# Accumulator banks and a split second layer for the last MLPs, a head set up in timed steps, and a new order of the last slots

## The chip, the cores and the metric

The kernel runs on one core of a Trainium2 chip. The metric is the device time in microseconds (us) of that core. TensorE is called PE here, VectorE DVE, ScalarE ACT, GpSimd POOL and SyncE SP.

## The reference, cut to what matters

The input x has the shape (4, 64, 64, 256), all in float32. Two layers follow one another.

```python
# layer 0: attention over the 4096 pixels of each image
q, k, v = x @ wq + bq, x @ wk + bk, x @ wv + bv          # 32, 32 and 256 columns
x = gamma * softmax(q @ k.T) @ v + x
# layer 1: a deformable 3x3 convolution (DCNv3, 16 groups) and an MLP, both with residuals
h  = ln(x)
xp = h @ inproj_w + inproj_b                              # what is sampled
d  = gelu(ln(depthwise_conv3x3(h)))
offset, mask = d @ off_w + off_b, softmax(d @ mask_w + mask_b)
s  = sum over 9 taps of mask * bilinear(xp, position + offset)
x  = x + s @ outproj_w + outproj_b
h  = ln(x)
x  = x + gelu(h @ fc1_w + fc1_b) @ fc2_w + fc2_b          # 256 -> 1024 -> 256
```

## The kernel before, in words

**Units and slots.** Each image is cut into 16 units of 256 pixels, 64 units in all. The work is cut into small steps, each a closure that issues a few instructions, and every step has a due time. A slot is 60 units of that time. Unit s has its attention in slot s and its `front` (residual, layer norm, input projection) in slot s+1. Convolution and sampling work on blocks v = 0 to 64, which are shifted by half a unit, so that the first and the last have one tile of 128 pixels and the others have two. Block v has its `plan` (convolution, offsets, masks, weights) in slot v+1, and its `sample` (weighted sums over a 5x5 window on DVE) and `back` (output projection, layer norm and MLP) in slot v+2. The last three blocks, 62 to 64, use `summing` in place of `sample`: part of the adding is then done on PE (`sum`, line 1093). A `far` step at the end repairs, through gathers, up to one sample in each of 128 rows that fell outside the window.

**The order.** `whole` (line 1372) collects all steps with their due times, from the table `WHEN` and, for the last slots, from the table `LATE` (from line 399), sorts them and calls them. Four engines (PE, DVE, ACT and POOL) execute their instructions strictly in that order. SP is not among them: it issues nearly all DMAs, in an order that the scheduler of the framework finds. The due times set an order only; nothing waits for a clock.

**The head.** Before the first step the kernel loads `raw_qk`, then, three times, the weights of offsets and masks into a buffer `raw` of one slot (lines 164 to 170, on SP), which `ordered` (lines 153 to 161) copies on DVE into `om_w` and `om_b` with another order of columns. The next load of `raw` has to wait for the copy before. POOL writes zero borders to the padded image `xp` in DRAM (lines 179 to 187, 16 DMAs) and zero halves (lines 201 to 203, 4 DMAs), and POOL and DVE together fill small tables (`numbers`, lines 212 to 241). Then the projections of the 16 units of the first image run one after another: load `xs` (line 617), transpose on PE (line 316), copy on ACT (line 624), keys on PE (line 630), key bias on ACT with a store `qd` from the two-slot buffer `qT` (lines 638 to 645), values on PE (line 651), value bias on DVE (line 659). `xs` has 8 slots then. Weights of the later stages are loaded on ACT's queue, one step each.

**The tail.** `finish` (line 1126) is the shared end of a block: transpose, output projection, layer norm, then eight `hidden` steps (line 1167; each fills one 128-row piece of the hidden layer in PSUM), eight `gelu` steps (line 1175, ACT reads that bank), and `narrowed` (line 1182), which multiplies all eight pieces with fc2 in one go. `back` (line 1211) and `far_round` (line 1249) use it. The PSUM pool `ps` has two banks with the tag `m`, shared by transposes, projections, `hidden` and `narrowed`. Four banks `e0` to `e3` belong to the attention energies, and two, `acc0` and `acc1` (pool `ps_a`), to the attention output; once the last attention is over, nothing uses these two.

Of the kernel before, what the change touches and what calls it, by code (L numbers as in the profile page):

```python
# [16 lines left out]
def tile_attention_dcnv3_block(  # L17
# [76 lines left out]

    def loaded(t, src, now=False):
        if now:
            nc.scalar.dma_start(t, src)
        else:
            loads.append(lambda: nc.scalar.dma_start(t, src))
# [62 lines left out]

    for k in range(C // P):
        raw = p1.tile([P, 2, NOM], F32, tag="om", name=f"raw_{k}")[:, 0, :]
        nc.sync.dma_start(raw[:, : 2 * S], off_w[k * P : (k + 1) * P, :])
        nc.sync.dma_start(raw[:, 2 * S :], mask_w[k * P : (k + 1) * P, :])
        ordered(om_w[:, k, :], raw[:, : 2 * S], raw[:, 2 * S :])
    raw = p1.tile([P, 2, NOM], F32, tag="om", name="raw_b")[:, 0, :]
    nc.sync.dma_start(raw[:, : 2 * S], off_b.partition_broadcast(P))
    nc.sync.dma_start(raw[:, 2 * S :], mask_b.partition_broadcast(P))  # L170
    ordered(om_b, raw[:, : 2 * S], raw[:, 2 * S :])
# [6 lines left out]
    for b in range(B):  # L178
        for y in (0, H + 2):
            nc.gpsimd.dma_start(  # L180
                xp[b, y : y + 2].rearrange("y w c -> (y w c)").rearrange("(p f) -> p f", p=P),
                zeros[:, : 2 * WP * C // P],
            )
        for w in (0, W + 2):
            nc.gpsimd.dma_start(
                xp[b, 2 : 2 + H, w : w + 2, :].rearrange("y w c -> y (w c)"), zeros[:H, : 2 * C]
            )

# [12 lines left out]
    for v in (0, UN):  # L201
        nc.gpsimd.dma_start(amd_[v, :, 1], zeros[:, :S])
        nc.gpsimd.dma_start(omd_[v, :, 1], zeros[:, :NOM])
# [14 lines left out]
    tab = p1.tile([P, WIN * C], F32, tag="acc", name="tab")  # L218
    byp = tab[0:1, : 6 * S].rearrange("p (s f) -> p s f", f=3)
    numbers(byp[:, :, 0], [[0, 2 * KP], [1, G]], 0)  # L220
    numbers(byp[:, :, 1], [[0, 2], [1, 3], [0, 3 * G]], -1)
    numbers(byp[:, :, 2], [[0, 6], [1, 3], [0, G]], -1)
    nc.gpsimd.dma_start(tab_s.rearrange("(o s) f -> o (s f)", o=1), tab[0:1, : 6 * S])
    tab = p1.tile([P, 2 * S], F32, tag="mk", name="tab_b")
    byt = tab[0:1, : 4 * UN].rearrange("p (s f) -> p s f", f=2)
    numbers(byt[:, :, 0], [[H + 4, B], [0, NT]], 0)
    numbers(byt[:, :, 1], [[0, B], [2, NT]], 0)
    nc.gpsimd.dma_start(tab_t.rearrange("(o s) f -> o (s f)", o=1), tab[0:1, : 4 * UN])
    tab = p1.tile([P, 2 * S], F32, tag="mk", name="tab_c")
    numbers(tab[0:1, :], [[1, 2 * S]], 1)  # L230
    nc.gpsimd.dma_start(tab_n.rearrange("(o s) -> o s", o=1), tab[0:1, :])

    where = gp.tile([P, 3], F32, name="where")
    numbers(where[:, 0:1], [[0, 1]], 0, 1)
    for r in range(2):
        numbers(where[r * W : (r + 1) * W, 1:2], [[0, 1]], 0, 1)
        nc.vector.memset(where[r * W : (r + 1) * W, 2:3], float(r))
    rev = gp.tile([P, PN], F32, name="rev")
    numbers(rev, [[-1, PN]], PN)
    g16 = gp.tile([P, G], F32, name="g16")  # L240
    numbers(g16, [[1, G]], 0)
# [69 lines left out]
    def transposed(src, name, n=2, pool=None, tag="m"):  # L311

        pt = (pool or ps).tile([P, C // P, 256], F32, tag=tag, name=f"pt_{name}")
        for k in range(C // P):
            for i in range(n):
# [57 lines left out]
            "narrowed0": 102.2, "narrowed1": 106.29, "end": 106.65,  # L373
# [7 lines left out]
            "hidden6": 52.93, "gelu6": 53.21, "hidden7": 53.49, "gelu7": 53.77, "narrowed0": 54.05,  # L381
            "end": 54.33,
# [17 lines left out]
        "attention": {  # L400
            60: {"e2": 41.63, "w7": 60.7, "x2": 61.55, "e3": 66.3, "w11": 68.16, "w10": 72.05, "x3": 77.04,
                "w4": 92.63, "w12": 96.73, "w14": 126.44, "w13": 147.54, "w6": 149.16, "w9": 151.58,
                "w8": 162.58, "w15": 163.18},
            61: {"load": 73.15, "e0": 77.73, "x0": 99.75, "e1": 104.68, "w0": 119.31, "x1": 120.96,
                "w4": 128.82, "w7": 135.45, "e2": 139.75, "w5": 140.73, "x2": 142.59, "w6": 144.13,
                "w9": 144.35, "e3": 145.78, "w11": 147.04, "w10": 148.04, "x3": 148.67, "w3": 150.79,
                "w13": 152.23, "w14": 153.3, "w2": 155.04, "w1": 159.09, "w12": 159.2, "w8": 161.6,
                "w15": 162.84},
            62: {"load": 99.58, "e0": 109.75, "x0": 110.1, "e1": 115.56, "w0": 118.27, "w2": 120.32,
                "x1": 120.74, "w6": 125.15, "e2": 126.82, "w5": 128.98, "x2": 130.87, "w7": 131.07,  # L410
                "e3": 132.81, "w11": 137.28, "w10": 140.15, "w1": 141.18, "x3": 141.21, "w3": 142.52,
                "w14": 145.25, "w4": 147.03, "w13": 147.58, "w12": 147.88, "w8": 148.09, "w9": 149.05,
                "w15": 151.71},
            63: {"load": 96.28, "e0": 109.66, "x0": 111.02, "w0": 116.5, "w1": 120.49, "e1": 121.69,
                "x1": 130.68, "w4": 132.65, "w5": 134.09, "e2": 139.76, "w2": 143.15, "w3": 145.56,
                "w6": 148.75, "x2": 149.1, "w10": 151.15, "e3": 151.17, "w7": 152.54, "w8": 159.2,
                "x3": 160.16, "w14": 161.32, "w12": 166.1, "w9": 172.0, "w13": 173.2, "w11": 173.78,
                "w15": 178.59},
        },
        "plan": {  # L420
            60: {"tap3": 42.14, "tap4": 45.5, "tap5": 45.93, "tap6": 48.85, "tap7": 56.79, "tap8": 69.29,
                "turn": 71.67, "stats": 84.78, "shift": 119.53, "norm": 125.14, "turn2": 134.12,
                "gelu": 136.3, "heads0": 139.79, "heads1": 139.85, "bias0": 140.11, "bias1": 141.55,
                "hat0": 143.63, "hat2": 145.22, "mask_exp": 149.39, "hat1": 152.25, "sums": 155.5,
                "nearer": 155.85, "invert": 159.93, "weigh": 161.42, "near": 162.49, "mask0": 163.69,
                "bounds": 164.12, "product0": 169.57, "y_copies0": 169.58, "mask1": 170.65, "y0": 170.84,
                "product1": 173.04, "carry": 176.72, "y_copies1": 176.81, "y1": 177.14, "x_copies": 177.7,
                "x": 179.94, "count": 186.05},
            61: {"tap0": 134.62, "tap1": 137.24, "tap2": 142.14, "tap3": 143.54, "tap4": 145.54,
                "tap5": 147.02, "tap6": 147.16, "tap7": 151.6, "tap8": 153.16, "turn": 155.38,  # L430
                "stats": 159.07, "shift": 163.55, "norm": 165.46, "turn2": 169.08, "gelu": 169.8,
                "heads0": 171.11, "bias0": 173.2, "heads1": 173.5, "bias1": 174.96, "mask_exp": 175.54,
                "sums": 176.03, "hat0": 176.77, "hat2": 179.12, "invert": 179.39, "hat1": 181.33,
                "weigh": 182.69, "nearer": 182.7, "carry": 184.49, "near": 184.56, "mask0": 186.43,
                "product0": 189.28, "mask1": 189.69, "y_copies0": 189.79, "y0": 189.8, "product1": 191.98,
                "y_copies1": 192.03, "y1": 193.12, "bounds": 193.14, "x_copies": 195.14, "x": 197.47,
                "count": 222.68},
            62: {"tap0": 130.69, "tap1": 130.86, "tap2": 132.89, "tap3": 137.61, "tap4": 138.36,
                "tap5": 140.21, "tap6": 143.86, "tap7": 145.27, "tap8": 146.85, "turn": 149.25,
                "stats": 154.57, "shift": 157.76, "norm": 160.13, "turn2": 162.96, "gelu": 163.59,  # L440
                "heads0": 170.06, "bias0": 170.97, "heads1": 171.09, "bias1": 171.17, "mask_exp": 171.28,
                "hat0": 174.71, "hat2": 175.31, "sums": 176.21, "carry": 179.99, "hat1": 180.81,
                "invert": 182.18, "nearer": 182.58, "weigh": 183.33, "near": 185.92, "mask0": 190.13,
                "mask1": 193.9, "product0": 196.16, "y_copies0": 201.23, "y0": 201.65, "product1": 204.17,
                "y_copies1": 207.73, "y1": 208.43, "x_copies": 210.39, "x": 210.97, "count": 221.66,
                "bounds": 346.38},
            63: {"tap0": 141.15, "tap1": 142.22, "tap2": 142.73, "tap3": 143.79, "tap4": 145.1,
# [147 lines left out]
                "summed0": 541.21},  # L595
        },
        "checks": {
            66: {"range": 530.02, "left": 563.34, "largest": 1080.93},
        },
    }  # L600

# [449 lines left out]
    def sample(v, wns, sps):  # L1051
# [71 lines left out]
        return d  # L1123


    def finish(x1, sp, name, n=2, after=None):
        m = n * P
        st = {}

# [366 lines left out]
```

## Time and profile before

| | |
|---|---|
| median of 3 runs | 3838.01 us (3837.57 to 3839.95) |
| the profiled execution | 3837.92 us |
| its span | 3835.8 us |
| PE busy | 3789.8 us, 99% of the span |
| DVE busy | 3401.7 us, 89% |
| ACT busy | 2199.0 us, 57% |
| POOL busy | 312.9 us, 8% |
| last attention matmul ends | about 3663 us |

The profiled execution lies 0.09 us under the median, and 2.1 us of it lie outside the span. A row of a table by stage gives, for a stretch of the span, the busy time of each engine with the number of instructions in brackets, the granted clock of PE as a share of full speed, the share of the 16 DMA engines' time in use, and what they moved. A row of a timeline gives the start, the duration, the engine, the line, the operation with output and input, the number of instructions, and in brackets the idle time before it with what ended that.

### The profile page before, as it was taken

How to read it: one execution, taken by the hardware profiler on the slowest of the kernel's cores; microseconds unless marked ns; L12 is line 12 of the kernel's file. 1: busy time of each engine (PE TensorE's matmuls, PEld its weight loads, DVE VectorE, ACT ScalarE, POOL GpSimd, SP SyncE). 2: the span in 40 equal slices, each digit the busy share in tenths (PEclk: the TensorE clock that was granted, in tenths of full speed). 3: DMA queues.
4: the chain of work that ended last, by engine and by line, in shares of the span. 5: the costliest groups of instructions: out<-in, count | busy, mean ns of one | idle time of the engine just before them, and what ended most of it. 6: DMA issues, size and time to landing. Idle time of an engine off the chain costs nothing.

```text
span 3835.8 us, 56185 instructions
## 1 busy us (share of the span) xinstructions
PE 3789.8 (99%) x20466; PEld 3139.2 (82%) x20466; DVE 3401.7 (89%) x6199; ACT 2199.0 (57%) x4261; POOL 312.9 (8%) x444
## 2 busy tenths in 40 slices
PE   8999999999999999999999999999999999999988
PEld 7788888888888888888888888888888888888867
DVE  2599899999998998998998999999999999999995
ACT  4556556565565565565565565655655565555543
POOL 1000000000000000000000000000000000000021
PEclk9999999999999999999999999999999999999999
DMA  5333333334343333333533333333344333333331
GB/s 151 91 102 90 96 96 93 99 90 139 97 112 92 102 92 90 106 92 90 149 99 105 97 92 99 91 95 97 100 127 112 91 86 88 98 84 84 88 93 51
DMA packets 231789, 378.03 MB, mean 99 GB/s; under 512 B 32880, under 2 KB 181936, under 8 KB 231504
## 3 DMA queue, kind: packets, MB, share of 16 engines
q1 hardware_dynamic: 221408, 367.46, 34.5%
q10 hardware_dynamic: 8512, 3.43, 0.4%
q8 instruction: 163, 2.67, 0.3%
q0 software_dynamic: 1584, 3.47, 0.3%
q14 instruction: 122, 1.00, 0.1%
HBM read 251.69 MB, written 122.56 MB: 98 GB/s over the span
## 4 chain that ended last, share of the span: by engine, by line
PE 96%; DVE 3%; DMA 1%; ACT 0%; issue 0%; SPq 0%; ACTq 0%; DVEq 0%
PE acc L744 46%; PE ph L1170 11%; PE pmlp L1187 11%; PE e L719 7%; PE po L885 5%; PE pout L1145 3%; PE pp L801 3%; PE pv L651 3%; PE pkq L630 1%; DVE pw L1064 1%; PE pt_p L316 1%; PE pc L861 1%; PE pt_f L316 1%; PE pt_s L316 1%; PE pt_b L316 1%; PE pt_x L316 1%
## 5 line engine op out<-in xcount | busy, mean ns | idle before, releaser
L744 PE MATMUL acc<-V,ex 128*128 128x257 f32 x8192 | 1900.9, 382 | 0.2
L744 PEld LDWEIGHTS acc<-V,ex 128*128 128x128 f32 x8192 | 1532.0, 190 | 264.5 <-issue 64.8
L1064 DVE TENSOR_TENSOR pw<-win,wn 128x1280 f32<-128x1280 f32 x640 | 933.8, 1486 | 9.5 <-ACT wn L1008 1.9
L1072 DVE TENSOR_TENSOR pw<-pw,pw 128x1280 f32<-128x1280 f32 x492 | 731.9, 1488 | 0.1
L732 ACT ACTIVATE ex<-e 128x512 f32<-128x512 f32 x1024 | 529.3, 602 | 63.0 <-PE e L719 54.2
L1170 PE MATMUL ph<-hT_b,f1w 128*128 128x256 f32 (+1 forms) x2080 | 493.2, 380 | 6.3 <-ACT gT L1178 2.8
L1187 PE MATMUL pmlp<-f2w,gT 128*128 128x256 f32 x2048 | 462.7, 379 | 1.3 <-DVE x1b L1152 1.1
L1170 PEld LDWEIGHTS ph<-hT_b,f1w 128*128 128x128 f32 x2080 | 381.9, 190 | 82.8 <-issue 18.9
L848 DVE SCALAR_TENSOR_TENSOR cv<-hs,dw,cv 128x256 f32<-128x256 f32 (+1 forms) x1076 | 429.9, 467 | 7.9 <-ACT cv L844 1.3
L1187 PEld LDWEIGHTS pmlp<-f2w,gT 128*128 128x128 f32 x2048 | 384.2, 190 | 51.8 <-DVE x1b L1152 1.4
L288 ACT ACTIVATE xn_p<-pc,nm_p,rstd_p 128x256 f32<-128x256 f32 x128 | 65.4, 560 | 554.1 <-DVE nm_p L280 551.2
L1178 ACT ACTIVATE gT<-ph,f1b 128x256 f32<-128x256 f32 (+1 forms) x520 | 236.5, 468 | 254.8 <-PE ph L1170 253.3
L719 PE MATMUL e<-qs,kT 32*128 32x256 f32 x4096 | 296.3, 401 | 0.7 <-ACT ex L732 0.7
L719 PEld LDWEIGHTS e<-qs,kT 32*128 32x128 f32 x4096 | 186.7, 184 | 72.3 <-issue 63.3
L732 ACT ACT_TABLE_LOAD x182 | 233.5, 1283 | 3.0
L274 POOL TENSOR_SCALAR rstd_p<-mv_p 128x2 f32<-128x2 f32 (+1 forms) x65 | 76.1, 1171 | 1703.4 <-DVE mv_p L272 1632.4
L885 PE MATMUL po<-om_w,ge 128*128 128x432 f32 x512 | 196.6, 527 | 0.7 <-ACT ge L878 0.7
L974 DVE TENSOR_TENSOR pr<-hat 128x1296 f32<-128x1296 f32 x128 | 192.7, 1505 | 0.6 <-DVE nm_b L280 0.5
L1178 ACT ACT_TABLE_LOAD x124 | 159.1, 1283 | 2.1
L878 ACT ACTIVATE ge<-pt_p,bd,gd 128x256 f32<-128x256 f32 (+1 forms) x130 | 66.0, 558 | 157.0 <-PE pt_p L316 157.0
L885 PEld LDWEIGHTS po<-om_w,ge 128*128 128x128 f32 x512 | 96.9, 190 | 71.1 <-issue 63.3
L894 DVE TENSOR_TENSOR om<-po,om_b 128x432 f32<-128x432 f32 x128 | 77.3, 605 | 87.3 <-PE po L885 87.3
(219 smaller groups left out, 3883.1 us busy)
## 6 DMA issues: line engine op xcount, KB each, us to landing
win<-xp SPq DMA_DIRECT2D x536, 320.0 KB, 4.1
omd<-om SPq DMA_DIRECT2D x63, 432.0 KB, 2.5
xs<-in_x_dram SPq DMA_DIRECT2D x64, 256.0 KB, 5.4
x<-in_x_dram SPq DMA_DIRECT2D x64, 256.0 KB, 2.7
x1d<-x SPq DMA_DIRECT2D x64, 256.0 KB, 3.2
xp<-xq SPq DMA_DIRECT2D x128, 128.0 KB, 2.4
x1b<-x1d SPq DMA_DIRECT2D x63, 256.0 KB, 2.8
spd<-sp SPq DMA_DIRECT2D x63, 256.0 KB, 2.1
```

The costliest lines, as they stand in the source:

```text
L316: nc.tensor.transpose(pt[:, k, i * P : (i + 1) * P], src[:, i, k * P : (k + 1) * P], ident)
L719: nc.tensor.matmul(es[r][:, jj, :], lhsT=self.kT[2 * g + jj][rows4(r), :], rhs=self.qs[rows4(r), :], start=True, stop=not self.general,)
L732: nc.scalar.activation(ex, self.es[r], AF.Exp)
L744: nc.tensor.matmul(self.acc[i], lhsT=ex[:, jj, i * P : (i + 1) * P], rhs=V[t // 2][:, t % 2, :], start=(g == 0 and r == 0 and jj == 0), st ...
L848: nc.vector.scalar_tensor_tensor(dst, src, dw[:, k, j : j + 1], dst, ALU.mult, ALU.add)
L885: nc.tensor.matmul(st["po", i], lhsT=st["ge"][:, k, i * P : (i + 1) * P], rhs=om_w[:, k, :], start=(k == 0), stop=(k == 1),)
L974: nc.vector.tensor_mul(pr.rearrange("p a b c d g -> p a b (c d g)"), hat[:, :, i, 1, :].unsqueeze(1).to_broadcast([P, 3, 3, S]), hat[:, :, ...
L1064: nc.vector.tensor_mul(st[r].rearrange("p d (g c) -> p (d g) c", c=GC), src.rearrange("p d (g c) -> p (d g) c", c=GC), wns[v][:, i, r] .re ...
L1072: nc.vector.tensor_add(st[0], st[0], st[r])
L1170: nc.tensor.matmul(ph[:, :m], lhsT=f1w[:, k, c * P : (c + 1) * P], rhs=st["hT"][:, k, :m], start=(k == 0), stop=(k == 1),)
L1178: nc.scalar.activation(st["gT"][:, c, :m], st["ph", c][:, :m], AF.Gelu, bias=f1b[:, c : c + 1])
L1187: nc.tensor.matmul(po, lhsT=st["gT"][:, c, i * P : (i + 1) * P], rhs=f2w[:, c, :], start=(c == 0), stop=(c == NH - 1),)
```

## The change

1. **Free banks.** `finish` gets an argument `last`. It is set for blocks 63 and 64 and for `far`. There, `hidden` takes its bank from a list of two, `acc0` and `acc1`, and `gelu` gives it back. The ring still has two banks, but it no longer shares them with transposes and projections.
2. **Split second layer.** Where `last` is set and the block has one tile (block 64 and `far`), the one step `narrowed0` becomes eight steps `part0` to `part7`, one for each piece of the hidden layer, with due times of their own. The matmuls are the same.
3. **Head in steps.** The three loads of `raw` with their copies, the borders, the halves and the tables are no longer issued ahead of the first step but become steps of their own: load and copy at -24 and -10, at -9 and 5, at 6 and 20; borders at -8, 1, 10 and 19; halves at 28; tables at 32. The projection of unit u of the first image has its value bias at about 3.6u - 59.5, so that the first copy stands between the value biases of units 13 and 14 in DVE's order, and the second and third after the last of them. The first energies of the attention are due at -5.06.
4. **New order.** All of `LATE` is replaced: the due times of the steps of slots 59 to 66.

```diff
+    head = []
+    def head_raw(t, offs, masks, dst):
+        st = {}
+        def load():
+            st["raw"] = raw = p1.tile([P, 2, NOM], F32, tag="om", name="raw_om")[:, 0, :]
+            nc.sync.dma_start(raw[:, : 2 * S], offs)
+            nc.sync.dma_start(raw[:, 2 * S :], masks)
+        head.append((t, load))
+        head.append((t + 14.0, lambda: ordered(dst, st["raw"][:, : 2 * S], st["raw"][:, 2 * S :])))
     for k in range(C // P):
-        raw = p1.tile([P, 2, NOM], F32, tag="om", name=f"raw_{k}")[:, 0, :]
-        nc.sync.dma_start(raw[:, : 2 * S], off_w[k * P : (k + 1) * P, :])
-        nc.sync.dma_start(raw[:, 2 * S :], mask_w[k * P : (k + 1) * P, :])
-        ordered(om_w[:, k, :], raw[:, : 2 * S], raw[:, 2 * S :])
+        rows = slice(k * P, (k + 1) * P)
+        head_raw(-24.0 + 15.0 * k, off_w[rows, :], mask_w[rows, :], om_w[:, k, :])
+    head_raw(6.0, off_b.partition_broadcast(P), mask_b.partition_broadcast(P), om_b)
...
+    for b in range(B):
+        head.append((-8.0 + 9.0 * b, lambda b=b: borders(b)))
...
+    head.append((28.0, halves))
...
+    head.append((32.0, tables))
...
+    spare = [0, 1]
-    def finish(x1, sp, name, n=2, after=None):
+    def finish(x1, sp, name, n=2, after=None, last=False):
...
         def hidden(c):
-            st["ph", c] = ph = ps.tile([P, 256], F32, tag="m", name=f"ph_{name}_{c}")
+            if last:
+                st["bank", c] = k = spare.pop(0)
+                ph = ps_a.tile([P, C + 1], F32, tag=f"acc{k}", name=f"ph_{name}_{c}")
+            else:
+                ph = ps.tile([P, 256], F32, tag="m", name=f"ph_{name}_{c}")
+            st["ph", c] = ph
...
+            if last:
+                spare.append(st["bank", c])
...
+        def part(c):
+            if c == 0:
+                st["pm"] = ps.tile([P, 2, C], F32, tag="m", name=f"pmlp_{name}")
+            nc.tensor.matmul(
+                st["pm"][:, 0, :], lhsT=st["gT"][:, c, :P], rhs=f2w[:, c, :],
+                start=(c == 0), stop=(c == NH - 1),
+            )
...
+            steps += [(t, len(steps) + i, fn) for i, (t, fn) in enumerate(head)]
```

In the new order of the last block, PE does hidden 0, 1 and 6, part 0, hidden 7, 3, 4 and 2, part 1, hidden 5, and parts 2 to 7; before, it did eight hidden steps and then `narrowed0`. Parts 6 and 7 of `far` stand between the last transpose of block 64 and its first hidden step.

## The prediction

> **What bounds the kernel.** I read the page's first part, then a table by stage. PE is busy 99% of the span, and from 260 to 3500 us without a gap, so no step there can be made shorter by another order.
>
> ```profile
> PE 3789.8 (99%) x20466; PEld 3139.2 (82%) x20466; DVE 3401.7 (89%) x6199; ACT 2199.0 (57%) x4261; POOL 312.9 (8%) x444
> ```
>
> ```profile
> 0.00:20.00 20.00, 12.15 (x43) 9.64 (x44) 5.07 (x39) 5.65 (x11) 12.36 (x27) 1.00 0.80 254
> 20.00:40.00 20.00, 16.53 (x85) 13.83 (x84) 7.87 (x20) 8.12 (x20) 3.91 (x13) 1.00 0.83 247
> ...
> 80.00:100.00 20.00, 20.00 (x125) 16.10 (x124) 0.00 (x0) 10.70 (x19) 0.00 (x0) 1.00 0.03 9
> ...
> 3600.00:3660.00 60.00, 59.88 (x321) 48.51 (x320) 59.02 (x115) 28.17 (x56) 8.41 (x11) 1.00 0.33 87
> 3660.00:3700.00 40.00, 31.34 (x128) 23.60 (x127) 36.94 (x82) 20.09 (x43) 8.21 (x8) 0.91 0.27 74
> 3700.00:3720.00 20.00, 16.94 (x80) 13.88 (x78) 19.45 (x62) 3.81 (x8) 4.95 (x7) 1.00 0.29 68
> 3720.00:3740.00 20.00, 17.88 (x80) 13.76 (x78) 20.00 (x42) 12.01 (x23) 2.44 (x2) 1.00 0.52 149
> ```
>
> The change adds and removes no PE work: eight parts hold the matmuls of one `narrowed0`. What it can win is PE's idle time, 3835.8 - 3789.8 = 46 us. By stage: 7.85 + 3.47 = 11.3 us up to 40 us; 6.7 us between 60 and 260 us, which the change does not touch; some 17 us between 3663 and 3825 us; and 10.8 us after PE's last matmul, which stay. In 3600 to 3760 us DVE is full, so there PE waits for DVE, not for banks. That last fact limits the new order most.
>
> **The head.** The timeline of PE shows three waits after the start:
>
> ```profile
> 21.86 1.99 PE L651 MATMUL pv<-wv_s,xT 128*128 128x256 f32 x8 [1.42 <-DVE V L659]
> ...
> 28.04 1.13 PE L630 MATMUL pkq<-xT,wkq 128*128 128x256 f32 x4 [0.72 <-ACT xT L624]
> ...
> 32.66 1.13 PE L630 MATMUL pkq<-xT,wkq 128*128 128x256 f32 x4 [1.32 <-ACT xT L624]
> ```
>
> The first has this cause: DVE stands in `ordered` until the bias loads land (20.11 us), with V's add queued behind. The others come from SP. There the reload of `raw` waited for a DVE copy and was issued at 14.43, with two loads of `xs`, further ones and the first store `qd` behind it; `qd` went out at 19.26, though its `qT` was written by 12.4. ACT needed that slot of `qT` and waited for the store:
>
> ```profile
> 26.16 0.73 ACT L638 ACTIVATE kT<-pkq,bkq 32x128 f32<-32x128 f32 x2 [5.91 <-DMA qd<-qT]
> ```
>
> With the three `raw` loads out of the way, both holds go: 1.42 + 0.72 + 1.32 = **-3.46 us**. What is late next is the store `qd` itself: by my reading it is issued near 16.5, behind the `xs` load that waits for the third unit's transpose (15.44 + 0.60), and landing takes 2.4 us in the median and 6.4 in this case (25.7 - 19.3). So it lands at 19 to 23, and ACT needs the slot at 20 to 21; I leave 0.2 us for it. **Head: -3.3 us.**
>
> PE's start hardly moves. The first `xs` load may go out 1.05 us earlier (1.75 for 2.80), but the values of unit 0 wait for `wv_s` (issued on ACT's queue at 4.61, landed at 11.86). More `xs` loads are then in flight beside it. The nearest row is the span of landing times of 256 KB loads in this head, 3.3 to 8.2 us, so `wv_s` could land between 3.9 us earlier and 1.0 later; I take no change, since its own row is 7.2. Bounds of the head: the start -2 (past that, ACT's first copy at 8.46 and `bv_s` bind) to +1, the waits -3.46 to 0.
>
> [...]
>
> **What moves at no cost.** The borders and halves: POOL has nothing ahead of them in its own order (its next work is `rstd_f` at 106.7 us), so their new due times delay them by nothing, and they stay in the way as now. The tables: ten DVE casts (about 2.6 us) and ten iotas now follow DVE's last value bias, in 65 to 100 us, where DVE does nothing (0.00 busy in 80 to 100). Without that cover they cost their ping-pong from 24.6 to 38 us, some 13 us of DVE. The copies into `om_w` and `om_b` take 6 x 0.40 us, two of them between value biases that stand 3.03 us apart and last 0.69. Their reloads on SP wait for DVE; if SP's order puts later `qd` stores behind one, ACT waits as at 39.81 (2.2 us), where PE lost nothing. `om_w` is first read near 130 us.
>
> **The tail, after the last attention (3663 us).** I wrote out both orders and summed rows.
>
> 1. *To the last `front`.* PE's next need from DVE is the transpose of `xn_f`. Between, PE has 13.4 us before (seven hidden of 0.865, one transpose 0.44, two `narrowed` of 3.46) and 12.1 after (six hidden, two `narrowed`). DVE has 18.3 us from L767 to L280 before and 14.3 after (two multiplies or adds and one product of 1.4 each fewer, `stats` 1.0 more, small ones either way). But `end` of block 59, which needs `narrowed1`, and one `across` now stand just ahead of that `shift`, so PE's gap is 0.55 + 0.6 + 0.6 + 0.1 + 1.0 = 2.9 us. The row before:
>
> ```profile
> 3682.70 1.40 PE L316 MATMUL pt_f<-ident,xn_f 128*128 128x128 f32 x4 [3.02 <-ACT xn_f L288]
> ```
>
> DVE must first have done 4 us more by 3663 than now, and it had 6.5 idle us since 3500. If it has, -1.5; if not, +1.1. I take 0.
>
> 2. *3689 to 3711.* Idle before: 0.91 + 1.11 + 0.56 + 0.56 + 1.15 + 1.82 = 6.1. After, by the walk: project-out directly behind its transpose (ACT's copy, 0.9), a bank freed by DVE's store (0.9), hidden directly behind its transpose (1.1), `gelu2` of block 60 queued on ACT behind `x_copies` of plan 62, which wait for DVE's `y1` (3.1), and the transpose of plan 63 for the last tap (1): 7.0, so **+0.9** (-2.2 if `y1` is early).
>
> 3. *3711 to 3745.* Before 1.11 + 0.66 + 0.35 + 1.13 = 3.3. After: `narrowed0` of block 61 waits for a bank that DVE frees late (2.6), and small ones (0.7): 3.3. **0**, between -2 and +1.
>
> 4. *3745 to 3825, the part that the new steps serve.* The wait for `hT_b` ahead of the last MLP (0.55 at 3815.95) is covered by two parts of `far` (2 x 0.43), and a wait of 0.30 for `sT` by hidden steps: -0.85. The last MLP now:
>
> ```profile
> 3815.95 4.79 PE L1170 MATMUL ph<-hT_b,f1w 128*128 128x128 f32 x32 [0.55 <-ACT hT_b L296]
> 3820.75 3.72 PE L1187 MATMUL pmlp<-f2w,gT 128*128 128x256 f32 x16
> ```
>
> At the rate of `ph_f` (0.89 for eight) the 32 would take 3.5 us: 1.3 are lost in the ring of two banks. The new ring also has two, so the waits stay, but part 0 and part 1 fill 2 x 0.43 of them: -0.9 (0 to -1.3). Parts 2 to 7 stand behind the last hidden step, where `narrowed0` stood.
>
> **Tail: 0 + 0.9 + 0 - 0.85 - 0.9 = -0.85 us** by the walk. A walk of this kind adds every new wait singly, and some fall together. Going through to the end in one piece (DVE and PE side by side from the last `front`), I get 141 us against 143.1 measured, so -2.1. I take the mean, **-1.5**, with ends -9 and +6.
>
> One price I can't settle: behind the wait of 3.02 us the granted clock is half, and `pp` takes 3.78 us in place of 1.73.
>
> ```profile
> 3682.70:3689.00 6.30, 5.37 (x13) 3.41 (x13) 4.23 (x10) 4.94 (x13) 0.00 (x0) 0.50 0.12 42
> ```
>
> That costs (1.40 - 0.44) + (3.78 - 1.73) = 3.0 us per such gap; 1.8 us at 3710 cost nothing like it. My gaps of 2.9, 3.1 and 2.6 lie near the edge: -3 to +6 us, inside the ends above.
>
> [...]
>
> **Sum:** 3837.9 (the profiled execution) - 3.3 - 1.5 = 3833.1; it stands 0.1 under the median, so 3833.2, a change of -0.13%.
>
> **Rivals.** Measurement of this kernel tells a change of about 0.2% (7.7 us) from none.
>
> - *As above*, 3833: both parts work but small. Chance 0.50.
> - *More is won*: the start is 1.5 us earlier, the holds go (-3.5), and the new order gets DVE's 4 us done early (-1.5), hides the wait on `x_copies` (-3), keeps the last front's gap short of the half clock (-3): -12.5, so 3825. For it: 14.9 us of PE idle between 3663 and 3745 are there to be had, DVE has 6.5 idle us ahead. Against: DVE at 59.0 of 60. Chance 0.42.
> - *Slower*: DVE comes late to the last `front`. The order asks 4 us more of it there; if it is 8 us late instead, this passes through (DVE is full until 3760), and two gaps beyond 3 us pay the half clock: +8 + 6 - 1.75 - 3.3 = +9, so 3847. It decides from about 7 us late. Against: DVE's remaining work there is 122 us after and 126 before. Chance 0.08.
> - *The change doesn't do what it says*: borders and ring unchanged, SP still holds `qd` behind another wait, tail by the walk: -0.85, so 3837. It is part of the first case's chance.
>
> **Chances.** Faster by over 0.2% (under 3830.3): the second case, and a little of the first, 0.43. Within: 0.49. Slower: 0.08. Range: 3821 (the second case with 4 us more of its bounds) to 3841 (the first with the head lost and the walk's upper bounds).
>
> **What would show it.** Right: no PE wait on V or `xT` in 20 to 33 us, the first energies near 62 us in place of 65.3; PE's last matmul 1 to 3 us earlier relative to the last `front`; hidden and part rows mixed in the last 10 us; DVE full from 3600 to 3760. Wrong: energies still at 65 (SP holds `qd`), or earlier than 60 (the start moved); PE idle of 3663 to 3745 under 9 us or over 20; half clock in more than one stretch there.

## The result, and the profile after

The changed kernel takes 3833.75 us (median of 22 runs, 3831.99 to 3837.05), the kernel before 3838.61 (22 runs, 3837.01 to 3842.84): a ratio of 0.9986, with a 95% interval of 0.9980 to 0.9993, or -4.9 us. The forecast was 3833.2. The profiled execution took 3833.11 us, its span 3831.2.

The page's first part of the changed kernel, and its table by stage:

```profile
PE 3790.6 (99%) x20466; PEld 3141.2 (82%) x20466; DVE 3401.8 (89%) x6199; ACT 2203.0 (58%) x4265; POOL 313.8 (8%) x444
```

```profile
0.00:20.00 20.00, 11.86 (x42) 9.15 (x43) 4.75 (x35) 5.42 (x11) 12.26 (x27) 1.00 0.88 304
20.00:40.00 20.00, 18.90 (x100) 16.46 (x99) 4.25 (x7) 10.54 (x25) 0.00 (x0) 1.00 0.84 211
...
3660.00:3700.00 40.00, 30.98 (x116) 23.82 (x115) 37.90 (x94) 17.34 (x39) 11.80 (x13) 0.83 0.26 78
3700.00:3720.00 20.00, 19.87 (x94) 16.37 (x93) 19.02 (x56) 8.43 (x18) 7.30 (x6) 1.00 0.32 85
```

PE idles less in 20 to 40 us (1.1 us in place of 3.5) and in 3700 to 3720 us (0.1 for 3.1), and the clock is lower around 3680 (0.83 for 0.91). The timeline of PE in the head, and the row of ACT that holds it:

```profile
12.25 3.78 PE L686 MATMUL pv<-wv_s,xT 128*128 128x256 f32 x8 [1.41 <-DMA wv_s<-in_L_conv_wv_dram]
...
26.95 1.13 PE L665 MATMUL pkq<-xT,wkq 128*128 128x256 f32 x4 [1.10 <-ACT xT L659]
...
62.62 1.15 PE L754 MATMUL e<-qs,kT 32*128 32x256 f32 x16
```

```profile
25.83 0.47 ACT L679 ACTIVATE qT<-pkq,bkq 32x256 f32<-32x256 f32 x1 [3.43 <-DMA qd<-qT]
```

The wait on V is gone, one wait on `xT` is left, and the first energies stand at 62.62 for 65.30. In the last slots:

```profile
3678.18 0.33 PE L335 MATMUL pt_f<-ident,xn_f 128*128 128x128 f32 x1 [2.09 <-ACT xn_f L307]
...
3679.95 3.78 PE L836 MATMUL pp<-inw,hT_f 128*128 128x256 f32 x8 [0.66 <-ACT hT_f L315]
...
3696.61 5.13 PE L1213 MATMUL ph<-hT_b,f1w 128*128 128x256 f32 x16 [3.30 <-ACT gT L1221]
...
3739.50 8.86 PE L1232 MATMUL pmlp<-f2w,gT 128*128 128x256 f32 x32 [1.69 <-DVE x1b L1189]
```

```profile
3811.86 1.85 PE L1213 MATMUL ph<-hT_b,f1w 128*128 128x128 f32 x12
3813.55 0.60 PE L1240 MATMUL pmlp<-f2w,gT 128*128 128x256 f32 x2
...
3816.92 2.76 PE L1240 MATMUL pmlp<-f2w,gT 128*128 128x256 f32 x12
```

The gap ahead of the last front is 2.09 us, shorter than forecast, and `pp` still takes 3.78. The last MLP runs without a wait. On this one profile the sum looks right in its parts too: head -2.7 (forecast -3.3), tail -2.1 (forecast -1.5). The experiments show that this agreement is luck.

### The profile page after: what moved, and what is told of

Read it like the earlier page. It is cut to its first block, busy times and chain, and to the rows that moved or that the text cites. A ratio compares the mean times of both kernels' runs of the same rounds, so it can differ in the third digit from the quotient of the medians.

```text
span 3831.2 us, 56200 instructions
## 1 busy us (share of the span) xinstructions
PE 3790.6 (99%) x20466; PEld 3141.2 (82%) x20466; DVE 3401.8 (89%) x6199; ACT 2203.0 (58%) x4265; POOL 313.8 (8%) x444
## 4 chain that ended last, share of the span: by engine, by line
PE 92%; DVE 3%; issue 0%; ACT 0%; POOL 0%; DVEq 0%; ACTq 0%; POOLq 0%
PE acc L779 44%; PE ph L1213 11%; PE pmlp L1232 11%; PE e L754 7%; PE po L920 5%; PE pout L1182 3%; PE pp L836 3%; PE pv L686 2%; PE pkq L665 1%; DVE pw L1099 1%; DVE cv L883 1%; PE pt_p L335 1%; PE pt_s L335 1%; PE pt_b L335 1%; PE pc L896 1%; PE pt_f L335 1%
## 5 line engine op out<-in xcount | busy, mean ns | idle before, releaser
L754 PEld LDWEIGHTS e<-qs,kT 32*128 32x128 f32 x4096 | 186.2, 184 | 72.8 <-issue 64.9
```

What stands on the lines that cost most here:

```text
L754: nc.tensor.matmul(es[r][:, jj, :], lhsT=self.kT[2 * g + jj][rows4(r), :], rhs=self.qs[rows4(r), :], start=True, stop=not self.general,)
```

## The experiments

Medians are of 8 or 11 runs, beside 12 to 33 of the kernel before in the same series (3838.55 to 3838.76). The table cuts each profile in two: from the first energies to the last front's transpose (`pt_f`), and from there to `pt_any`, PE's last matmuls; "half spans" are explained below the third experiment.

| kernel | first energies | to `pt_f` | to the end | half spans (60 to 80 us / tail) | median |
|---|---|---|---|---|---|
| before | 65.30 | 3617.40 | 141.70 | 0 / 2 | 3838.61 |
| changed | 62.62 | 3615.56 | 141.43 | 0 / 5 | 3833.75 |
| head_only | 63.60 | 3619.16 | 141.68 | 1 / 2 | 3838.36 |
| raw_only | 64.36 | 3621.27 | 142.18 | 2 / 3 | 3841.21 |
| tail_only | 64.13 | 3617.79 | 138.36 | 1 / 1 | 3833.73 |
| old_order | 65.48 | 3619.44 | 141.16 | 1 / 3 | 3838.88 |
| banks_no_split | 65.29 | 3617.83 | 140.85 | 1 / 2 | 3836.91 |
| gelu_early | 66.71 | 3617.88 | 139.58 | 1 / 2 | 3834.21 |
| fill | 65.51 | 3618.86 | 138.23 | 1 / 2 | 3835.59 |
| qT4 | 62.64 | 3617.85 | 138.87 | 1 / 2 | 3834.19 |
| qd_on_act | 64.45 | 3620.58 | 140.04 | 2 / 2 | 3836.28 |
| start | 62.92 | 3616.41 | 140.04 | 0 / 2 | 3832.60 |
| best3 | 61.37 | 3618.30 | 138.86 | 1 / 2 | 3833.62 |
| borders_late | 57.59 | 3615.54 | 141.46 | 0 / 5 | 3828.67 |

**1. The halves apart: head_only, tail_only, raw_only.** `head_only` is the kernel before with the head in steps; `tail_only` the changed kernel with the head issued first, as before; `raw_only` is `head_only` with only the `raw` loads in steps.

```diff
 head_only:  old LATE, and no last=...
 tail_only:  -        head.append((t, load))
             +        load()
             (and the same for the other four head.append)
 raw_only:   head_only, with borders(b), halves() and tables() called in place
```

> The head in timed steps alone; banks, parts and the order of the last slots as before. My theory: the head is worth 2.7 us by itself (first energies 65.30 to 62.62 us in the two profiles), because the reloads of the raw weights no longer stand in SP's order ahead of the qT stores nor in DVE's ahead of the V adds; the last slots then take what they took before, so the time is 3838.6 - 2.7 = 3835.9 us, first energies at 62.6, and from there to PE's last matmul 3759.7 us as before. Rival: the head gains nothing of its own at the end because a later wait (the transposes between 60 and 260 us, or the last slots) takes it back: 3838 us with energies at 62.6. Second rival: the order of the last slots is worth all of it and the head shifts with the run: energies at 65.

> Banks, parts and the new order of the last slots alone; the head issued ahead of the first step as before. My theory: -2.1 us (from the first energies to PE's last matmul 3757.6 us after for 3759.7 before): 3836.5 us, first energies at 65.3. The sum with the other half then adds up to the whole change, -4.9. Rival: the two halves help one another (the DMA rows or DVE's state at 3600 us differ), so that this half alone gives under 1 us or over 4.

> Only the three loads of the raw weights with their copies become timed steps; borders, halves and tables stand ahead of the first step, and the last slots are as before. My theory: all of the head's gain comes from these three, so the first energies are at 62.6 within 0.5 and the time is 3835.9 us. Rival: the casts of the tables on DVE (ten, with ten iotas on POOL, from 24.6 to 38 us before) held V adds too, or the small writes of the borders held loads; then the energies come at 63.5 to 65 and half of the gain or more is missing.

Measured against the kernel before: `head_only` 1.0000 (0.9991 to 1.0009), `tail_only` 0.9989 (0.9980 to 0.9998), `raw_only` 1.0005 (0.9996 to 1.0014). So the last slots bring all of the 4.9 us that can be seen. The head brings none that can be told: 0.4 us without the new order and 0.0 beside it. Taken run by run, the mean differences are -0.3 us (95% interval -1.6 to 1.2) and -0.4 (-1.9 to 0.9). My theory of -2.7 for the head lies outside both and fell, and that of -2.1 for the tail with it. The first energies tell why one profile misled: with the same new head they came at 62.62, 63.60, 65.48, 65.51, 66.71 and 65.29 (mean 64.9), with the old head at 65.30 and 64.13 (64.7). The profiled execution of the changed kernel was the earliest of six. Its wait on `xT` was also the shortest of the six; in the four with waits of 2.5 us or more the granted clock then fell to half between 26 and 34 us. The theory on `raw_only` fell too (energies at 64.36, no gain). Its median is 2.8 us over `head_only`; the two intervals above overlap, but run by run the mean difference is 2.2 us (0.6 to 3.8), so something seems lost where borders, halves and tables stay ahead. What it is stays open.

**2. The order and the split apart: old_order, banks_no_split.**

```diff
 old_order: changed kernel, old LATE, with
 66: "part0": 756.0, "part1": 863.2, "part2": 884.1, "part3": 942.92 ... "part7": 943.32   (block 64)
 66: "part0": 631.85 ... "part7": 632.55                                                   (far)
 banks_no_split: "part7": 1123.25 -> "narrowed0": 1123.25, "part7": 781.47 -> "narrowed0": 781.47
```

> The head in timed steps, the free banks and the parts, but with the old order of the last slots; part 0, 1 and 2 of the last block stand behind gelu 6, 2 and one more in the old order, parts 3 to 7 where the one step stood. My theory: the new order of 3663 to 3745 us was worth nothing (its losses and gains cancel), and the banks and parts alone give 0.9 of the last slots' 2.1 us (the last MLP 9.45 to 8.6 us), the rest being the wait on hT_b and the ring that the order hides: 3838.6 - 2.7 - 0.9 = 3835.0 us. Rival: the order is what gains, and banks and parts give nothing without it: 3835.9 us and a last MLP of 9.4 us. Second rival: the new order loses, and this kernel is faster than the changed one: under 3833.

> The changed kernel without the split: the second layer of block 64 and of far is one step again, where part 7 stands. All else is the changed kernel's. My theory: the split is worth the waits that the parts fill (hT_b 0.55, sT 0.30, two parts of the ring's waits 0.9): 1.0 to 1.8 us, so 3834.8 to 3835.5 us, and from the last gelu to the end of the second layer 3.5 us in place of 2.8. Rival: ACT's gelus bind that stretch whatever PE does; then only the parts behind the last gelu count, and the loss is under 0.5 us.

`old_order` has the ratio 0.9997 (0.9988 to 1.0006): without the new order, banks and parts show nothing in the median, though its last MLP (first `ph` to `pt_any`) took 7.91 us for 8.45 before. My theory of 3835.0 fell; the first rival was right on the time, not on the last MLP. `banks_no_split` lost 3.2 us against the changed kernel, for the 1.0 to 1.8 of my theory. By the table 1.35 of them stand behind `pt_f`, against the mean of the five profiles with equally many half spans and the parts (gelu_early, qT4, qd_on_act, start, best3: 139.5); where the rest is, the profiles don't show. Its timeline shows what the parts had covered:

```profile
3812.29 0.44 PE L335 MATMUL pt_b<-ident,xn_b 128*128 128x128 f32 x2 [1.01 <-ACT xn_b L307]
...
3816.02 4.56 PE L1213 MATMUL ph<-hT_b,f1w 128*128 128x128 f32 x32
3820.42 3.62 PE L1232 MATMUL pmlp<-f2w,gT 128*128 128x256 f32 x16
```

`pt_b` waits 1.01 us for `xn_b`, where otherwise parts of `far` stand. The MLP itself takes 7.95 us, nearly what it takes with parts (7.75), for 8.45 before: in these profiles most of its gain comes with the free banks, little with parts inside it. The new order without the free banks wasn't tried: there, as I read the order, hidden steps of one block stand among transposes and hidden steps of others, and with two shared banks a step would wait for a bank that only a later step frees.

**3. The half clock: fill.** Behind the same wait of 1.69 us `pmlp` took 8.86 us in the changed kernel's profile and 7.17 in that of `tail_only`. A table in steps of 0.05 us shows why: in each profile the clock changes only on a grid of 3.41 us of its own. In the changed kernel it turns to half at 166.69, 3679.01, 3696.08 and 3740.45 us, which lie 1029, 5 and 13 whole steps of 3.413 us apart; the half stretches that its trace records up to PE's last matmul last 3.413, 10.240, 3.413 and 3.413 us, those of the kernel before 6.827 and 6.827. Cut on that grid:

```profile
3675.61:3679.02 3.41, 1.15 (x7) 0.52 (x5) 2.85 (x7) 1.10 (x2) 0.00 (x0) 1.00 0.23 78
3679.02:3682.43 3.41, 2.75 (x8) 2.04 (x7) 3.00 (x19) 3.06 (x7) 1.26 (x2) 0.50 0.24 77
...
3692.67:3696.09 3.42, 0.64 (x3) 0.21 (x2) 3.42 (x12) 0.46 (x3) 0.92 (x2) 1.00 0.00 0
3696.09:3699.50 3.41, 2.89 (x7) 2.36 (x8) 3.41 (x9) 1.30 (x4) 0.00 (x0) 0.50 0.23 77
...
3737.05:3740.46 3.41, 1.52 (x7) 1.14 (x7) 3.41 (x9) 0.58 (x3) 0.00 (x0) 1.00 0.00 0
3740.46:3743.87 3.41, 3.41 (x9) 2.70 (x8) 3.13 (x13) 1.06 (x3) 1.89 (x4) 0.50 0.02 5
```

The first column after the length is PE's busy time, the last but two the clock. A span with 1.15, 0.64 or 1.52 us of PE work (34, 19 and 45%) is followed by one at 0.50. Over all 14 profiles 2281 spans of 8 to 260 and 3480 to 3790 us were cut so, each on its own grid, and none was mixed. (In the traces of the changed kernel and the kernel before, the record of the clock begins at 16.5 us, and the tables show 1.00 ahead of it, though eight matmuls of `pv` took 3.78 us at 12.25 and 1.89 at 17.47; what follows counts spans from some 18 us on.) 45 spans at full clock with PE busy up to 45% were followed by a half span; above that, none was, apart from ten spans that hold the first energies (52 to 89% busy; matmuls of 32 rows). The lowest that stayed full were busy 45 and 48%. From half, the clock came back behind spans busy 83% or more and stayed behind 82% or less (two spans with energies apart). A half span takes 1.71 us of PE's full clock (half of 3.413). How many a gap of 2 us makes depends on where the grid falls, and that differs from profile to profile.

```diff
+    def fill():
+        pf = ps_e.tile([P, 256], F32, tag="e2", name="fill")
+        for i in range(8):
+            nc.tensor.matmul(pf, lhsT=ident, rhs=f1w[:, 0, :256], start=True, stop=True)
...
+            steps.append((64 * T + 193.05, len(steps), fill))
```

> The changed kernel, with eight more matmuls of 128x256 (the identity by a piece of fc1, into an energy bank that nobody reads) just ahead of the transpose of the last front, in PE's idle 2.09 us there. My theory, from the six profiles so far: the clock is set anew every 3.41 us on a fixed grid, half where PE was busy less than some 45 to 50% of the span before, and one such span costs 1.7 us of PE. The gap of 2.09 us makes one to three half spans, by where the grid falls. Filled with 8 x 0.22 = 1.73 us, it leaves 0.36: no half span between 3676 and 3690, pp at 1.7 to 1.9 us for eight and not 3.78, and the median 1 to 2 us under the changed kernel's 3833.75. Rival: the clock falls for another reason (the end of the attention, a change of the kind of work); then the half spans stay and the median is the same or up to 0.4 above.

```profile
3680.92 3.62 PE L1433 MATMUL fill<-f1w,ident 128*128 128x256 f32 x16
3684.37 0.60 PE L335 MATMUL pt_f<-ident,xn_f 128*128 128x128 f32 x4
```

No half span lies between 3676 and 3690, where each of the other 13 profiles has one that begins between 3674 and 3688, and `pp` takes 2.02 us: the half span went with the gap, as I had expected. But I had sized the fill wrongly: each of these float32 matmuls stands as two records of 0.226 us, so eight took 3.62 us and `pt_f` came some 1 us late (3618.86 in the table). The median is 1.8 us worse, not better, and two half spans came at 3691 and 3701 instead.

**4. A new wait in the last slots: gelu_early.**

```diff
-  62: "gelu2": 353.17, "gelu1": 354.07
+  62: "gelu2": 343.9, "gelu1": 343.95
```

> The changed kernel, with gelu 2 and gelu 1 of block 60 moved up in ACT's order, ahead of the copies of plan 62 that wait 3.13 us for DVE. PE waits 3.30 us for these gelus (at 3696.61). My theory: that wait goes, and with it the half span behind it: PE's last matmul comes 3 to 4 us earlier after the last front's transpose than the changed kernel's 141.4 us, and the median is 2.5 to 4 us lower, 3830 to 3831. Rival: DVE binds these slots (busy 37.9 of 40 us in 3660 to 3700), PE waits later for the same DVE work, at the sum or the adds behind: the waits move to 3720 to 3745 and the median gains less than 1 us.

The wait fell from 3.30 to 1.20 us, and another came right behind:

```profile
3701.87 1.99 PE L1213 MATMUL ph<-hT_b,f1w 128*128 128x256 f32 x8 [1.20 <-ACT gT L1221]
3706.48 1.21 PE L896 MATMUL pc<-ident,cv 128*128 128x128 f32 x4 [2.62 <-DVE cv L883]
```

In the 28 us behind `pt_f` PE idles 7.8 us here, 7.0 to 7.7 in the others with two half spans and the new order (without `fill`), and 6.7 in the kernel before: by all that these rows show, DVE (busy 37.9 of 40 us) sets that stretch, whichever wait is moved. The median (3834.21) is the changed kernel's. The rival was right.

**5. What holds the head: qT4, qd_on_act, start, best3, borders_late.**

```diff
 qT4:           four slots for qT in the first image (two of tag "qT", two of tag "x1b")
 qd_on_act:     -            nc.sync.dma_start(qd[b * NU + u], qT[rows, :])
                +            queue = nc.scalar if first else nc.sync
                +            queue.dma_start(qd[b * NU + u], qT[rows, :])
 start:         wv_s and bv_s loaded ahead of the key biases, these on nc.gpsimd
 best3:         start and qd_on_act
 borders_late:  start, and
                -    nc.vector.memset(zeros, 0.0)
                +    head.append((-29.0, lambda: nc.vector.memset(zeros, 0.0)))
```

> The changed kernel, with four slots for qT in the first image in place of two, so that ACT need not wait until the store qd has landed. The head alone was worth 0.4 us (3838.36 for 3838.76) and nothing beside the new order (3833.75 with it, 3833.73 without). My theory: the waits on V went, but the wait on the store stayed (ACT 3.4 to 4.3 us at 25.8 to 27.0, PE 1.1 to 2.5 on xT), since eight loads of xs at once fill SP until 10 us and the store goes out at 17.8 to 18.5 and lands near 26. With four slots no PE wait on xT is left between 20 and 36 us, the first energies come at 61 to 63 us, and the median is 1 to 2 us lower, near 3832.3. Rival: the loads themselves bind the head (DMA share 0.84 to 0.88); then PE waits for xs or wv_s as much longer, and neither the energies nor the median move.

> The changed kernel, with the stores qd of the first image issued on ACT's queue in place of SP's. In the eight profiles with the new head the first store goes out at 17.8 to 18.5 us behind some 13 loads of 256 KB on SP and lands near 26, as it did in the kernel before, where it went out at 19.3; PE waits 1.1 to 4.7 us for it on xT. My theory: the store is late because of the loads ahead of it on SP's queue. On ACT's queue it goes out near 12.5 and lands within some 4 us; no PE wait on xT of over 0.5 us is left between 20 and 36 us, the first energies come at 60.5 to 62 us (mean of the new head so far 64.9), and the median is 2 to 3.5 us under 3833.75. Rival: the DMA engines are full (share 0.88) and serve what is old first whatever the queue: the store still lands after 23 us and the median is the same.

> The changed kernel, with the loads of wv_s and bv_s first on ACT's queue and the eight small loads of the key biases moved from ACT's queue to POOL's. ACT's table load then no longer stands behind ten DMA issues (6.84 us). My theory: xT of the first unit comes 2 to 4 us earlier and the first pv near 9 us in place of 11.1 to 12.6, but the store qd still lands near 26, so that PE waits on xT as much longer: first energies and median gain under 1 us. Rival: the start is what bounds the head, and all 3 us come through.

> Both: wv_s first, key biases on POOL's queue, the stores qd of the first image on ACT's. My theory: with the store's wait gone, the early start comes through: first pv near 9 us, no wait on xT, first energies at 57.5 to 59.5 us, and the median 5 to 6.5 us under the changed kernel's, 3827 to 3829. Rival: the loads of xs bind next (third and fourth unit not landed when PE wants them): waits on xs of 1 to 3 us and only half of the gain.

> The kernel with the early start (wv_s first, key biases on POOL's queue; 3832.6 us), with one edit more: DVE's clearing of the zeros that POOL's border writes read becomes a step between the value biases of units 8 and 9, so that these 2.1 MB and the loads of the first windows move from 2.6 to 20 us to some 38 to 55 us, where the DMA share is 0.1 to 0.4. All profiles so far show 390 to 400 GB/s from 12 to 24 us whatever the order of the queues. My theory: the head is bound by what the DMA engines must move before the stores and loads that PE waits for, not by the place in a queue; taking 2.1 MB out of 8 to 24 us (5.4 us at 390 GB/s) lets the first store land before 20 us: no PE wait of over 0.5 us between 12 and 36 us, first pv before 8.5 us, first energies at 57 to 60 us, and the median 2 to 4 us under 3832.6. Rival: the queues hold it (the store stands behind the loads of xs on SP, ACT behind its own DMA issues); then the waits of 1.6 to 2.5 us on xT stay, energies at 62 to 63 us and the median within 1 us.

`qT4`: the wait on `xT` moved to 30.00 (1.62 us), the median stayed (3834.19). `start`: the first `pv` came at 10.31, the first store went out at 12.74 and landed near 21.6 all the same (the first `qs`, which reads it, goes out at 21.56), and PE waited 2.54 us on `xT`; 3832.60. But this wait was no longer one for the store:

```profile
26.42 0.39 ACTq L101 DMA_DIRECT2D g<-in_L_conv_ln_g_dram  x1
26.86 0.73 ACT L673 ACTIVATE kT<-pkq,bkq 32x128 f32<-32x128 f32 x2 [4.15 <-DMA xs<-in_x_dram]
...
28.59 1.48 PE L665 MATMUL pkq<-xT,wkq 128*128 128x256 f32 x4 [2.54 <-ACT xT L659]
```

`kT` reads no `xs`. What waited is the issue of the small load `g`, which stands just ahead of it in ACT's order. That row names a load of `xs` as what ended ACT's idle time. The trace of the kernel before shows how such a load comes in. It gives with each transfer the number of a semaphore (a counter) that is raised as the transfer lands. The 83 transfers of the first 40 us have 16 numbers, eight for SP and ACT together and eight for POOL. 67 times a number was taken over there from an earlier transfer whose landing can be told, and each time the issue stands behind that landing, by as little as 0.016 us: `gamma_s` went out at 25.74, and the store that had its number before had landed at 25.72; `g` at 30.49, after a load of `xs` at 30.47. In the changed kernel's trace it is so 27 times of 27: `g`, say, went out at 27.23, and the second store, with the number before, had landed at 27.21. In `qT4`, `g` went out at 27.84, after 4.34 us of idle ACT; its row names no transfer.

`best3`: on ACT's queue the first store went out at 13.54 and had landed by 18.1, when the first `qs` went out: 4.6 us, where on SP's queue it took 8.8 in `start`. But ACT then stood at its own loads, `gamma_s` (out at 21.61, 4.85 us of idle, which by its row a load of `x` ended) and `g` (26.06, 2.31 us, ended by `gamma_s`), PE had waits of 1.65 and 1.19 us, and the median was 3833.62. `qd_on_act`: the store went out only at 17.37, though its `qT` was written at 12.31, and ACT was idle for 5.53 us there; what held the issue, no row shows. It landed by 23.6, waits of 1.11 and 0.49 us were left, `wv_s` came later (first `pv` at 13.17), and the median was 2.5 us worse. My theory that the store's place in the queue holds the head fell: when the store came earlier, in `best3`, another transfer was what ACT waited for. Four edits of slots and queues, and not one moved the median by more than 1.2 us for the better. Taking the small loads out of ACT's order in the head wasn't tried.

`borders_late` takes 2.1 MB of border writes out of the way, and with them the loads of the first windows, which wait for them. The table by 4 us of the changed kernel, then of `borders_late` (last column GB/s, before it the DMA share):

```profile
12.00:16.00 4.00, 3.75 (x9) 2.92 (x10) 0.00 (x0) 0.11 (x1) 2.47 (x5) 1.00 1.07 389
16.00:20.00 4.00, 4.00 (x23) 3.62 (x22) 1.30 (x2) 1.88 (x5) 1.22 (x3) 1.00 1.07 395
20.00:24.00 4.00, 4.00 (x23) 3.51 (x22) 0.78 (x2) 1.19 (x3) 0.00 (x0) 1.00 1.06 309
```

```profile
12.00:16.00 4.00, 4.00 (x25) 3.52 (x24) 0.96 (x2) 1.77 (x4) 0.00 (x0) 1.00 1.07 358
16.00:20.00 4.00, 4.00 (x23) 3.54 (x22) 1.12 (x2) 2.36 (x5) 0.00 (x0) 1.00 0.25 60
20.00:24.00 4.00, 4.00 (x23) 3.51 (x22) 0.69 (x1) 2.64 (x7) 0.00 (x0) 1.00 0.68 173
```

In the changed kernel the DMA engines run flat out (share 1.05 or more) from 8 to 24 us; the 390 to 400 GB/s that I had put to all profiles from 12 to 24 us are not there throughout (309 here from 20 to 24; 232 in the kernel before from 16 to 20). In `borders_late` they are through by 16, and PE has no wait between 12 and 36 us. Its timeline of POOL and PE:

```profile
39.26 1.13 POOL L189 DMA_DIRECT2D xp<-zeros  x2 [33.40 <-DVE zeros L183]
```

```profile
10.04 2.62 PE L686 MATMUL pv<-wv_s,xT 128*128 128x256 f32 x8
...
57.59 1.15 PE L754 MATMUL e<-qs,kT 32*128 32x256 f32 x16
```

The first store goes out at 12.35, as in `start`, and lands by 16.7 (the first `qs` goes out at 16.68) in place of 21.6; ACT waits for these stores only twice, 1.0 and 0.2 us; the first energies come at 57.59. The median is 3828.67 us (3828.11 to 3830.22), 3.9 under `start`, 5.1 under the changed kernel and 10.0 under the kernel before (0.9974, 0.9964 to 0.9985): the best version of this study. Whether the bytes of these writes count or the number of their packets, no run separates.

## Why the prediction was right, and where it was not

The time was right (3833.2 for 3833.75) by luck: it is the sum of two terms that were both wrong, in opposite directions.

- **Head, -3.3: wrong, measured about 0.** The step that failed is "So it lands at 19 to 23 [...]; I leave 0.2 us for it". SP did let the store go earlier (17.8 to 18.6 for 19.26; I had said 16.5), and DVE did let V through. But the store landed at 25.7 to 27.3, no sooner than before, and PE waited 1.1 to 4.7 us on `xT` (mean of six profiles 2.8), where the old head had waited 3.5 and 4.0 in all, on V and `xT` together. I had followed the order on SP and DVE, and not the bytes: with the DMA engines flat out (389 to 395 GB/s from 8 to 20 us), an earlier place for one transfer left another one late. I had even priced the limit away with "The borders and halves [...] stay in the way as now", which was true and was the bound: `borders_late`, where they are out of the way, has no such wait.
- **The row behind it: misread in part.** The row at 26.16 is `kT`, which needs no slot of `qT`. Just ahead of it ACT stood at the issue of `gamma_s`, which took over the store's semaphore (number 106 in the trace); the store landed at 25.72. The issue of `g` stands in the same way behind a load of `xs` (number 105, landed 30.47), and PE's wait of 1.32 us at 32.66 follows it, so that wait was not one for the store.

```profile
25.74 0.37 ACTq L99 DMA_DIRECT2D gamma_s<-in_L_conv_gamma_dram  x1
...
30.49 0.39 ACTq L99 DMA_DIRECT2D g<-in_L_conv_ln_g_dram  x1
```

- **My rival "SP still holds `qd` behind another wait": half right.** In the changed kernel `qT` was written at 12.11. SP issued the store at 17.80, and the transfer took 7.9 us more.
- **PE's start, 0: right.** The first `pv` came at 11.1 to 12.6 (mean of six 11.8) for 11.86. `wv_s`, on ACT's queue, took 7.1 us from issue to landing (5.10 to 12.21) for 7.2 before. The store on that queue still took 6.2 us in `qd_on_act` (17.37 to 23.6), with the DMA share at 1.07 to 1.09 from 16 to 24 us.
- **Tables, `raw` reloads, halves at no cost: right.** The casts and all iotas but the first stand at 72 to 81 us, reloads at 58 and 64 us, and PE has no wait from them.
- **Tail, -1.5: too small.** By the medians it is -5.0 (`tail_only`), by the profiles at equally many half spans -3.6. The parts, in us:

| step | forecast | measured | from |
|---|---|---|---|
| 1, to `pt_f` | 0 (-1.5 to +1.1) | -1.4 | mean to `pt_f`, less 1.71 for each half span of 60 to 80 us, without `fill`: 3616.2 for 3617.6 |
| 2, 28 us behind `pt_f` | +0.9 | +0.4 | PE idle 7.1 (`qT4`) for 6.7 |
| 3, the next 34 us | 0 | -1.1 | PE idle 2.3 for 3.4; the wait for a bank was 1.69, not 2.6 |
| between 3 and 4, 50 us | none | +0.4 | PE idle 1.4 for 1.0 |
| 4, the last 29 us | -0.85 | -1.0 | PE idle 0.02 for 0.98 |
| 4, the last MLP | -0.9 | -0.7 | 7.75 for 8.45; free banks alone brought 0.5, not the parts |

In step 1 the gap ahead of `pt_f` was 2.09 for the forecast 2.9, and DVE was not late. (Two of the profiles, the changed kernel's and `borders_late`, have one half span near 165 us where the others have two; without them step 1 is -1.2.) Steps 2 to 4 sum to -2.0, and the profiles at two half spans give -2.2 (139.5 for 141.7). The other 1.4 us of the medians lie within their interval; no profile shows them.

- **The price of a gap, 3.0 us beyond about 3 us: wrong.** The rows show no such edge. A gap cost whole half spans, by the share of PE's work in a span of the grid (up to 45%, as counted above). Gaps of 2.09 and 1.69 us paid in the changed kernel's profile, and in `tail_only` the 1.69 did not. The changed kernel's profile had five half spans of this kind in the tail, that of the kernel before two; the grid lies differently in every profile, and whether that is part of the spread of the 22 runs was not tested.
- **The signs to look for:** no wait on V: right; none on `xT`: wrong; energies near 62: right in one profile, mean 64.9; PE's last matmul 1 to 3 us earlier behind the last front: 0.3 in the changed kernel's profile, 2.2 in the mean of the five; hidden and part rows mixed: right; DVE full from 3600 to 3760: busy 152.6 of 160 us; half clock in more than one stretch, named as a sign against me: it came, and the time held; by two profiles a half span in the tail costs 0.8 us and not 1.71 (141.4 us with five, 138.4 with one). That DVE covers the rest is my reading, not tested.

## What to carry to other kernels

Where the DMA engines are full, an earlier place for one transfer can leave another one late, as here (store out at 17.80 for 19.26, landed at 25.74 for 25.72): count the bytes that must be through, and move out what nobody needs yet, before turning to the order of queues or to slots. An engine that issues loads in its own order can stand at such an issue, as ACT did here for 4.85 us in `best3`; look there before you put its idle time down to its inputs. When terms are a few us, one profile of each kernel can confirm a wrong split of a right sum; undo each half and compare medians, and cut several profiles at the same marks. Before a wait is taken away, find out which engine sets the stretch: in `gelu_early` what was won at one wait was lost at the next, with DVE busy nearly throughout.

## What I had not expected of the hardware

- In these 14 profiles the clock of PE changed only on a grid of 3.413 us, which lay differently in each: half behind a span with PE busy up to 45% (the lowest that stayed full were busy 45 and 48%), full again behind one busy 83% or more, with no mixed span in 2281.
- Ten spans with the first energies, busy 52 to 89%, were followed by half clock as well: they hold matmuls of 32 rows. Why they are an exception, no run shows.
- The issue of a small load held ACT for over 4 us (4.15 in `start`, 4.85 in `best3`). In the two traces with the semaphores' numbers no issue of the first 40 us stands ahead of the landing of the transfer that had its number before (67 of 67 and 27 of 27 that can be told).
- A 32 KB store took 8.8 us from issue to landing with the DMA engines full (`start`, 12.74 to 21.56, share 1.07 from 12 to 20 us), 4.6 us beside as full engines but on ACT's queue (`best3`, 13.54 to 18.1, share 1.06), and 4.3 us when they were nearly through (`borders_late`, 12.35 to 16.68, share 1.07 to 16 us and 0.25 behind).
